# A four-direction Mamba block with two quantized FFNs: where the C rows live, and when the next step's work is issued

## The chip, the core and the metric

The kernel runs on one core of a Trainium2 chip. A core has five engines with a queue each: TensorE (PE in the profile; its weight loads are PEld), VectorE (DVE), ScalarE (ACT), GpSimd (POOL) and the sync engine (SP), which here issues nearly all DMA transfers. The metric is the device time of one launch in microseconds (us), the median over runs.

## The reference, cut to what matters

Two images `x[2, 96, 128, 128]` pass through two layers. The first layer normalizes over channels and runs four Mamba scans: over the pixels row by row, the same backwards, column by column, and that backwards. The outputs are concatenated, projected by `fuse_w` and added to `x`. An FFN follows, whose products and sums are rounded to 8 and 16 bits. The second layer is a 3x3 convolution over the normalized image and another FFN. Nearly all time is in the four scans:

```python
# per direction: D_INNER = 192 channels, D_STATE = 16 states, L = 16384 positions
xc, z = jnp.split(x @ in_w.T, 2, axis=-1)
xc = silu(causal_conv_4_taps(xc) + conv_b)
xdbl = xc @ xproj_w.T                      # dt_raw (6), B (16), C (16) of each position
dt = softplus(dt_raw @ dt_w.T + dt_b)
A = -exp(A_log)
def step(h, t):                            # h[channel, state]
    dA = exp(dt_t[:, :, None] * A)
    h = dA * h + dt_t[:, :, None] * B_t[:, None, :] * u_t[:, :, None]
    y = einsum('bds,bs->bd', h, C_t)
y = (ys + Dp * xc) * silu(z)
out = y @ outp_w.T
```

## The kernel before, in words

For each image the kernel runs three stages: `normalize`, `mamba` and `ffn_and_conv`. The change touches only `mamba` and the layout of its weights.

`mamba` takes the directions in two pairs (0, 2) and (1, 3), `pi` 0 and 1. The two directions of a pair have 2x192 = 384 channels, which are three groups `g` of 128 partitions: group 0 belongs to the first direction, group 2 to the second, and group 1 holds 64 channels of each, interleaved partition by partition. A step is 512 positions of a pair; there are 32 steps per pair, 64 per image, 128 in all. A step has 24 units: 3 groups times 8 pairs of states. Two units whose states are neighbours share a quad, a tile of 128x4x512 elements (1 MB) that holds rows of B or of C for four states. Each row is the same for all channels of a direction, so a quad is a transfer from DRAM that repeats the rows over the partitions (L335).

For one unit:

- `b_part` (L339) multiplies a B quad by dt·u on GpSimd, for two units at once. Then L342 and L343 add the state at the step's entry: `entry` on ScalarE forms the decay of the first position (L303), GpSimd multiplies it by the stored state `hst` and adds it to the first column.
- `decay` (L349) computes exp(A·dt) on ScalarE, two states, into one of three PSUM tiles `da`.
- `scan` (L353) is a scan instruction on VectorE per state. Its result goes into `da`, or into the B quad if GpSimd will multiply it.
- `behind` comes one unit later: the product with C on VectorE (L441), or for the units in `BY_POOL` on GpSimd (L360); it is written over the C quad. Then ScalarE copies the last column into `hst` (L442).
- `sums` (L357) adds the products over the states on TensorE into the PSUM bank `y`, with an identity as weights. For a unit of GpSimd the sums are issued three units later.
- At the first unit of a group, `gated` (L364) multiplies the finished `y` of the group before by silu(z) on VectorE. `y` has one bank, so the next group's first matmul (L448) waits for the gate. `project` and `collect` follow some units later.

The next step's preparation, `prologue`, is spread between the units. Its list `at` gives each piece a place (unit, before or after the unit's scans), counted from the start of the step before: the load of the normalized input `xa` and `xb` (-3), convolutions with the input projection (`inproj`, L211, at 1, 5 and 9), `rows` for dt, B and C (12), their way to DRAM (14), dt (14 to 17), gates (7, 18, 21), SiLU and softplus, which need another function table. All matmuls of the preparation and of the projection go through one PSUM bank, `misc`: each waits until ScalarE has read out the one before.

Group 1's convolution and gate outputs are computed with the two directions in halves and then interleaved by two small transfers (`mix`, L256).

The order of the instructions on each engine is the order in which the program issues them (`in_order`). The buffers and the waits are set by the tile pools: a tile gets a buffer when an earlier tile is released, which is after the last use of that tile. A transfer on SP that has to wait for this holds up what is behind it. Before the change, B quads rotate over four buffers and are fetched three quads ahead (`B_AHEAD`), C quads over three, two ahead (`C_AHEAD`).

Of the kernel before, what the change touches and what calls it, by code (L numbers as in the profile page):

```python
# [10 lines left out]
F32 = mybir.dt.float32  # L11
# [12 lines left out]
T = 512  # L24
# [8 lines left out]
B_AHEAD = 3  # L33
C_AHEAD = 2
AHEAD = 2
BY_POOL = tuple((g, s) for g in range(3) for s in (0, 8))
# [5 lines left out]
def tile_metaformer(ctx: ExitStack, tc: tile.TileContext, a: dict, out: bass.AP):  # L42
# [142 lines left out]
    def mamba(acc, xnr, xnc):  # L185

        with ExitStack() as st:
            pool = lambda n, bufs, **kw: st.enter_context(tc.tile_pool(name=n, bufs=bufs, **kw))

            io, gen, one, mixp, two = (pool(*p) for p in (("io", 2), ("gen", 4), ("one", 1), ("mixp", 1), ("two", 2)))  # L190
# [4 lines left out]
            enter = one.tile([128, NG, S], F32, name="enter")  # L195
# [5 lines left out]
            def inproj(pi, g, w, src, taps):  # L201

                ps = misc()
                for k in taps:
                    se = {"start": k == taps[0], "stop": k == taps[-1]}
                    for d, rows, lo, hi in (
# [4 lines left out]
                        nc.tensor.matmul(ps[rows, :], w(PAIRS[pi][d], k, lo, hi), src[d][:, k : k + T], **se)  # L211
                return ps

            def prologue(pi, i, d):
# [17 lines left out]
                def conv(g):  # L232
                    d["ps"] = inproj(pi, g, lambda dd, k, lo, hi: inx[:, dd, k, lo:hi], src, (0, 1, 2, 3))

                def conv_out(g):
                    if g == 1:
                        d["xc"] = two.tile([128, NG, T], F32, name="xc")
                    t = mixed("xc") if g == 1 else d["xc"][:, g, :]
                    nc.scalar.activation(t, d["ps"], AF.Identity, bias=convb[:, pi, g : g + 1])  # L239

                def gate(g):
                    d["ps"] = inproj(pi, g, lambda dd, k, lo, hi: inz[:, dd, lo:hi], src, (3,))

                def gate_out(g):
                    if g == 1:
                        d["sz"] = two.tile([128, NG, T], F32, name="sz")
                    nc.scalar.copy(mixed("sz") if g == 1 else d["sz"][:, g, :], d["ps"])  # L247

                def mixed(name):
                    d["mix", name] = mixp.tile([128, T], F32, name="mix")  # L250
                    return d["mix", name]

                def mix(name):

                    for k in range(2):
                        nc.sync.dma_start(d[name][k:128:2, 1, :], d["mix", name][64 * k : 64 * k + 64, :])  # L256
# [44 lines left out]
                def entry(g):  # L301

                    nc.scalar.activation(enter[:, g, :], amat[:, pi, g, :], AF.Exp, scale=d["dt"][:, g, 0:1])  # L303

                first = pi == 0 and i == 0
                at = [(-3, 1, load), (3, 0, partial(mix, "xc")), (11, 0, partial(silu, "xc"))]
# [360 lines left out]
```

## Time and profile before

| What | Value |
|---|---|
| Median of 3 runs | 11546.39 us (11545.31 to 11548.33) |
| Profiled execution: time, span | 11556.77 us, 11555.0 us |
| Mean granted TensorE clock | 0.989 |
| TensorE, VectorE, ScalarE, GpSimd busy over the span | 90%, 90%, 68%, 84% |
| Moved by DMA | 3416.96 MB, mean 296 GB/s |
| Row quads from DRAM | 3072 transfers of 1024.0 KB |

Shares of the span are means over three kinds of stages. In the 40 slices of the page, GpSimd is at 9 tenths in the two long scan stages and at 1 or 2 in the FFN stages. A row of a group gives: source line, engine, operation, output and inputs, count, then busy time in us and the mean in ns of one, then the idle time of the engine before these instructions and what released them. A row of the timeline gives start and duration in us; `x2` means merged instructions, and brackets name an idle time and its releaser. A row of stretches gives the stretch, its length, busy time and count of PE, PEld, DVE, ACT and POOL, then the granted clock, the DMA engines' busy share and GB/s.

### The profile page before, as it was taken

The page shows a single profiled execution, that of the slowest core. Times are in us where ns is not written, and L with a number is a line of the kernel's source. Part 1 is how long each engine was busy: PE and PEld are TensorE (multiplying, and loading weights), DVE is VectorE, ACT ScalarE, POOL GpSimd, SP SyncE. Part 2 cuts the span into 40 slices and gives each one's busy share as a digit, 9 for nine tenths or more (in the row PEclk, how much of TensorE's full clock was granted, in tenths as well). Part 3 has the DMA queues.
Part 4 walks back from the last instruction along what each step waited for, and adds up shares of the span by engine and source line. Part 5 has one row for each costly group of instructions (what it writes and reads, how often), then busy time and mean ns, then how long its engine had stood idle before and what let it go on. Part 6 is the DMA issues. An engine that isn't in the chain of part 4 may idle for free. (4 is left out here: it accounts for less than half of the span.)

```text
span 11555.0 us, 94102 instructions
## 1 busy us (share of the span) xinstructions
PE 10435.0 (90%) x24208; PEld 3971.4 (34%) x24208; DVE 10421.6 (90%) x10127; ACT 7901.7 (68%) x13564; POOL 9672.3 (84%) x4700
## 2 busy tenths in 40 slices
PE   7999999999999999989989999999999999999899
PEld 2333333333333333333323333333333333333333
DVE  6999999999999999994469999999999999999944
ACT  6767767677677677665567677677676776776655
POOL 5999999999999999991159999999999999999911
PEclk8999999999999999999989999999999999999999
DMA  7888888888888888880068888888888888888800
GB/s 263 335 329 333 333 332 332 330 331 333 329 332 333 330 331 333 329 322 19 26 243 334 328 331 334 330 333 333 333 331 329 332 332 329 331 333 329 319 13 13
DMA packets 540755, 3416.96 MB, mean 296 GB/s; under 512 B 67532, under 2 KB 68652, under 8 KB 143832
## 3 DMA queue, kind: packets, MB, share of 16 engines
q1 hardware_dynamic: 539960, 3410.16, 76.8%
q8 instruction: 196, 3.21, 0.1%
q14 instruction: 343, 2.81, 0.1%
q0 software_dynamic: 256, 0.79, 0.0%
HBM read 3289.04 MB, written 54.53 MB: 289 GB/s over the span
## 5 line engine op out<-in xcount | busy, mean ns | idle before, releaser
L339 POOL TENSOR_TENSOR row<-dtu,row 128x2048 f32<-128x2048 f32 x1536 | 6948.9, 4524 | 283.3 <-DMA row<-bcd 281.6
L357 PE MATMUL y<-row,ident 128*128 128x512 f32 x12288 | 5690.6, 603 | 700.0 <-DVE row L441 699.9
L353 DVE TENSOR_TENSOR_SCAN da<-da,row 128x512 f32<-128x512 f32 x4608 | 5456.9, 1214 | 38.9 <-ACT da L349 5.2
L349 ACT ACTIVATE da<-dt,amat 128x512 f32<-128x512 f32 x6144 | 4246.9, 691 | 170.2
L357 PEld LDWEIGHTS y<-row,ident 128*128 128x128 f32 x12288 | 2256.8, 190 | 4008.4 <-issue 2243.5
L441 DVE TENSOR_TENSOR row<-da,row 128x1024 f32<-128x1024 f32 x2304 | 2776.7, 1205 | 70.2 <-DMA row<-bcd 70.0
L442 ACT COPY hst<-da 128x2 f32<-128x2 f32 x2304 | 368.9, 160 | 2652.2 <-DVE row L441 2649.3
L360 POOL TENSOR_TENSOR row<-row,row 128x1024 f32<-128x1024 f32 x768 | 1807.4, 2353 | 223.0 <-DVE row L353 147.5
L353 DVE TENSOR_TENSOR_SCAN row<-da,row 128x512 f32<-128x512 f32 x1536 | 1852.4, 1206 | 91.9 <-POOL row L339 84.1
L211 PE MATMUL misc<-xa,inx 96*64 96x512 f32 (+1 forms) x2048 | 946.1, 605 | 50.0 <-ACT mix L239 26.8
L211 PE MATMUL misc<-xb,inx 96*64 96x512 f32 (+1 forms) x2048 | 952.3, 608 | 33.6 <-ACT hst L442 24.2
L564 POOL TENSOR_TENSOR acc<-acc,y 96x512 f32<-96x512 f32 x128 | 147.4, 1151 | 991.5 <-DVE y L563 991.5
L298 POOL TENSOR_TENSOR dtu<-dt,xc 128x512 f32<-128x512 f32 x384 | 487.4, 1269 | 106.0 <-DMA xb<-xnc 99.8
L576 PE MATMUL pc<-pad,kw 96*96 96x512 f32 x1152 | 566.4, 593 | 0.0
L211 PEld LDWEIGHTS misc<-xa,inx 96*64 96x64 f32 (+1 forms) x2048 | 327.3, 165 | 581.2 <-issue 438.0
L448 PE MATMUL y<-xc,dmat 128*128 128x512 f32 x768 | 419.5, 628 | 103.6 <-DVE sz L364 103.6
L374 PE MATMUL misc<-sz,gmat 128*96 128x512 f32 x1024 | 484.1, 595 | 0.0
L284 PE MATMUL misc<-rows,dtw 12*128 12x512 f32 x768 | 434.3, 645 | 50.6 <-ACT dt L289 37.9
L364 DVE TENSOR_TENSOR sz<-y,sz 128x512 f32<-128x512 f32 x384 | 264.6, 689 | 229.5 <-PE y L357 198.0
L136 DVE TENSOR_TENSOR xq<-xm,rs 96x512 fp8e5<-96x512 f32 x128 | 87.9, 687 | 392.2 <-ACT rs L132 392.2
L211 PEld LDWEIGHTS misc<-xb,inx 96*64 96x64 f32 (+1 forms) x2048 | 316.5, 164 | 361.9 <-issue 214.1
L372 PE MATMUL misc<-acc,ident 96*96 96x512 f32 x512 | 387.6, 842 | 57.3 <-ACT sz L247 53.8
(76 smaller groups left out, 7449.9 us busy)
## 6 DMA issues: line engine op xcount, KB each, us to landing
row<-bcd SPq DMA_DIRECT2D x3072, 1024.0 KB, 7.4
xc<-mix SPq DMA_DIRECT2D x256, 128.0 KB, 5.4
sz<-mix SPq DMA_DIRECT2D x256, 128.0 KB, 8.9
xa<-xnr SPq DMA_DIRECT2D x124, 193.1 KB, 8.6
xb<-xnc SPq DMA_DIRECT2D x124, 193.1 KB, 8.7
bcd<-rows SPq DMA_DIRECT2D x128, 128.0 KB, 9.5
acc<-in_x_dram SPq DMA_DIRECT2D x16, 768.0 KB, 5.7
xnr<-xn SPq DMA_DIRECT2D x16, 768.0 KB, 4.3
```

The costliest lines, as they stand in the source:

```text
L211: nc.tensor.matmul(ps[rows, :], w(PAIRS[pi][d], k, lo, hi), src[d][:, k : k + T], **se)
L284: nc.tensor.matmul(d["ps"], w, d["rows"][0 : 2 * RK, :], start=True, stop=True)
L298: nc.gpsimd.tensor_tensor(dtu, d["dt"][:, g, :], d["xc"][:, g, :], ALU.mult)
L339: nc.gpsimd.tensor_tensor(b, d["dtu"][g][:, None, :].broadcast_to((128, 4, T)), b, ALU.mult)
L349: nc.scalar.activation(da[:, j, :], d["dt"][:, g, :], AF.Exp, scale=amat[:, pi, g, s + j : s + j + 1])
L353: nc.vector.tensor_tensor_scan(h[:, j, :], da[:, j, :], b[:, j, :], 0.0, ALU.mult, ALU.add)
L357: nc.tensor.matmul(y, ident, c[:, j, :], start=False, stop=s + j == S - 1)
L360: nc.gpsimd.tensor_tensor(c, h, c, ALU.mult)
L374: nc.tensor.matmul(d["po"], gmat[:, pi, 2 * g - 2 + k, :], d["yg"][g - 1 + k], start=False, stop=k == 1)
L441: nc.vector.tensor_tensor(c, h, c, ALU.mult)
L448: nc.tensor.matmul(y, dmat[:, pi, g, :], d["xc"][:, g, :], start=True, stop=False)
L576: nc.tensor.matmul(pc, kw[:, t, :], rows, start=t == 0, stop=t == 8)
```

## The change

- C has four fixed quads, `crow`, one for each four states. They are filled whole for group 0; for group 1 only partitions 64 to 127 are refilled (with the second direction's rows), for group 2 partitions 0 to 63. Each refill is issued two quads after the quad's use.
- Products are written over the B quad. B quads rotate over five buffers, four ahead, and are fetched after the unit's scans.
- Group 1 is laid out in two halves of partitions instead of interleaved: its B quad takes two transfers of 64 partitions, and the `mix` transfers go.
- The entry state: ScalarE multiplies the first column of the decay by `hst`, with two copies of 128x1 per unit, and the scan starts from 1. GpSimd's additions go.
- GpSimd multiplies 7 of 24 units by C: states 2 and 8 of each group and 4 of group 1 (before: 0 and 8).
- The next step's preparation is issued at other places: the load at -6, the convolutions at -3, -1 and 1, in halves of two taps before and after the unit's scans, rows at 6, dt at 8 to 10, softplus at 11, gates at 12, 14 and 16, SiLU at 5 and 21.

```diff
-B_AHEAD = 3
-C_AHEAD = 2
+B_AHEAD = 4
-BY_POOL = tuple((g, s) for g in range(3) for s in (0, 8))
+BY_POOL = tuple((g, s) for g in range(3) for s in (2, 8)) + ((1, 4),)
...
-                at = [(-3, 1, load), (3, 0, partial(mix, "xc")), (11, 0, partial(silu, "xc"))]
-                at += [(9, 0, partial(mix, "sz")), (31, 1, partial(silu, "sz"))]
-                at += [(12, 0, rows), (13, 1, rows_out), (14, 0, rows_to_dram)]
-                for g, k in ((1, 1), (0, 5), (2, 9)):
-                    at += [(k, 0, partial(conv, g)), (k + 1, 1, partial(conv_out, g))]
-                for g, k in ((1, 7), (0, 18), (2, 21)):
+                at = [(-6, 1, load), (5, 1, partial(silu, "xc")), (21, 1, partial(silu, "sz"))]
+                at += [(6, 0, rows), (7, 1, rows_out), (8, 0, rows_to_dram)]
+                for g, k in ((1, -3), (0, -1), (2, 1)):
+                    at += [(k, 0, partial(conv, g, (0, 1))), (k, 1, partial(conv, g, (2, 3))), (k + 1, 1, partial(conv_out, g))]
+                for g, k in ((1, 12), (0, 14), (2, 16)):
                     at += [(k, 0, partial(gate, g)), (k + 1, 0, partial(gate_out, g))]
-                soft = ((0, 1, 16), (1, 3, 26)) if first else ((0, 3, 17),)
-                for x0, x1, k in soft:
-                    at += [(k, 1, partial(softplus, x0, x1))]
-                for g, k in enumerate((14, 24, 25) if first else (14, 15, 16)):
-                    at += [(k, 0, partial(dt_in, g)), (k + 1, 0, partial(dt_out, g))]
-                for g, k in enumerate((19, 27, 29)):
+                for g in range(NG):
+                    at += [(8 + g, 0, partial(dt_in, g)), (9 + g, 0, partial(dt_out, g))]
+                at += [(11, 1, partial(softplus, 0, NG))]
+                for g, k in enumerate((13, 24, 26) if first else (13, 17, 21)):
                     at += [(k, 0, partial(dt_u, g))]
-                    if i > 0:
-                        at += [((20, 24, 29)[g], 1, partial(entry, g))]
...
+            def row_tile(d, g, s):
+
+                t = gen.tile([128, 4, T], F32, name="row", bufs=B_AHEAD + 1)
+                for part, k in (((slice(0, 64), 0), (slice(64, 128), 1)) if g == 1 else ((slice(0, 128), g // 2),)):
+                    src = d["bcd"][0, s // 4, k]
+                    nc.sync.dma_start(t[part], src[None].broadcast_to((part.stop - part.start, 4, T)))
                 return t
+            crow = [one.tile([128, 4, T], F32, name=f"crow{q}") for q in range(S // 4)]
+
+            def c_fill(n, g, q):
+
+                if n < len(steps):
+                    part = (slice(0, 128), slice(64, 128), slice(0, 64))[g]
+                    src = state[n]["bcd"][1, q, int(g > 0)]
+                    nc.sync.dma_start(crow[q][part], src[None].broadcast_to((part.stop - part.start, 4, T)))
...
+                if i > 0:
+                    for j in range(2):
+                        nc.scalar.activation(da[:, j, 0:1], da[:, j, 0:1], AF.Copy, scale=hst[:, g, s + j : s + j + 1])
                 return da
-            def scan(j, da, b, h):
-                nc.vector.tensor_tensor_scan(h[:, j, :], da[:, j, :], b[:, j, :], 0.0, ALU.mult, ALU.add)
+            def scan(i, j, da, b, h):
+                nc.vector.tensor_tensor_scan(h[:, j, :], da[:, j, :], b[:, j, :], float(i > 0), ALU.mult, ALU.add)
...
-                    nc.vector.tensor_tensor(c, h, c, ALU.mult)
+                    nc.vector.tensor_tensor(b, h, c, ALU.mult)
...
                 if k % 2 == 0:
-                    fetch(k + 2 * B_AHEAD, 0, B_AHEAD, bs)
                     feed(k + AHEAD)
...
                 if k % 2 == 0:
-                    fetch(k + 2 * C_AHEAD, 1, C_AHEAD, cs)
+                    fetch(k + 2 * B_AHEAD)
+                    if 4 <= k < total + 4:
+                        cn, cu = divmod(k - 4, nu)
+                        cg, cq = cu // 8, cu % 8 // 2
+                        c_fill(cn + (cg == 2), (cg + 1) % 3, cq)
                 issue(k, 1)
```

The weights' layout follows (no permutation of group 1), and the program's scratch for software DMA is set to 4096 bytes.

## The prediction

> **What bounds the kernel now.** I read the page, then the stretches, the groups, one step of the timeline, and the waits. The page and a stretch of 1000 us inside the scan stage:
>
> ```profile
> PE 10435.0 (90%) x24208; PEld 3971.4 (34%) x24208; DVE 10421.6 (90%) x10127; ACT 7901.7 (68%) x13564; POOL 9672.3 (84%) x4700
> 4000.00:5000.00 1000.00, 912.23 (x2106) 347.48 (x2106) 967.37 (x873) 701.82 (x1211) 939.76 (x456) 1.00 0.86 331
> ```
>
> In the stage VectorE is 96.7% busy, GpSimd 94%, TensorE 91%, the DMA engines 86%. The chain of waits shows the same `y` piece at 8521.24 and at 10818.34, 29 steps apart: 79.2 us a step, so 128 steps are 10,138 of the 11,555 us. The groups:
>
> ```profile
> L353 DVE TENSOR_TENSOR_SCAN da<-da,row 128x512 f32<-128x512 f32 x4608 | 5456.9, 1214 | 38.9 <-ACT da L349 5.2 <-POOL row L339 0.8 <-ACT hst L442 0.8
> L441 DVE TENSOR_TENSOR row<-da,row 128x1024 f32<-128x1024 f32 x2304 | 2776.7, 1205 | 70.2 <-DMA row<-bcd 70.0
> L364 DVE TENSOR_TENSOR sz<-y,sz 128x512 f32<-128x512 f32 x384 | 264.6, 689 | 229.5 <-PE y L357 198.0 <-ACT hst L442 16.5 <-ACT mix L247 13.0
> L343 POOL TENSOR_TENSOR row<-row,enter 128x4 f32<-128x4 f32 x1488 | 298.3, 200 | 116.6
> L342 POOL TENSOR_TENSOR enter<-enter,hst 128x16 f32<-128x16 f32 x372 | 82.3, 221 | 0.0
> ```
>
> VectorE's largest idle time stands before the gate (L364), which waits for a group's last sums. Queues within one step:
>
> ```profile
> 8529.55 1.21 DVE L441 TENSOR_TENSOR row<-da,row 128x1024 f32<-128x1024 f32 x1
> 8530.67 2.33 DVE L353 TENSOR_TENSOR_SCAN da<-da,row 128x512 f32<-128x512 f32 x2
> 8580.44 0.69 DVE L364 TENSOR_TENSOR sz<-y,sz 128x512 f32<-128x512 f32 x1 [1.15 <-PE y L357]
> 8521.24 5.42 PE L357 MATMUL y<-row,ident 128*128 128x512 f32 x12 [1.38 <-DVE row L441]
> 8553.82 3.70 PE L211 MATMUL misc<-xb,inx 96*128 96x512 f32 x8 [0.44 <-ACT hst L442]
> 8580.70 1.28 ACT L293 ACT_TABLE_LOAD   x1
> 8524.98 15.52 SPq L335 DMA_DIRECT2D row<-bcd  x5
> ```
>
> VectorE issues an operation every 1.12 us (the end is 1.21 after the start), a gate takes 0.60. The sums of one unit are 4 records: 1.75. A four-tap convolution of 8 records takes 3.44 (half: 1.72), group 1's of 16 took 3.6. ScalarE's function changes (load, softplus or SiLU, load) take 4.1. The sync queue's waits in the same 80 us, and a quad's landing:
>
> ```profile
> SPq L335 <- PE y L357: 54.0, 11, 9.4
> DMA to landing us min/median/max: 4.1/7.4/17.9
> ```
>
> The queue stands 54 of 80 us on TensorE's sums: a quad's buffer is refilled only when its sums are done. A step needs 48 scans, 18 products, 3 gates: 66×1.12+1.8 = 75.7; 3.5 us are stalls.
>
> [...]
>
> **The change, part by part.** *VectorE*: 17 products: −1.12 us a step. Also, unit s=0 is no longer GpSimd's, so a product of 1.12 stands between a group's last sums and its gate; that could remove the gate's waits (198.0+16.5+13.0)/128 = 1.8. *GpSimd*: one more product (+2.35), without 12 row and 3 state operations ((298.3+82.3)/128 = −3.0): −0.6, hidden, as VectorE hardly waits for it. The mix transfers (0.5 MB, four SP issues) go: hidden.
>
> *ScalarE*: two 128x1 copies per unit behind the exponentials. [...]I take 0.5 us per unit. Ends: 0.2 (two row copies stood 0.08 from the next operation) and 0.6. A decay (state copy 0.2, exponentials 1.42, copies 0.5) is 2.1; in steady state it hides in waits of 1.1 to 1.8, not behind a function change.
>
> *DMA*: C falls from 12 to 8 MB a step; B for group 1 goes in two 64-partition transfers, C refills for groups 1 and 2 in one each. A single quad's minimum of 4.1 is about 1.5 fixed plus 2.6 per MB. Half transfers lie between full rate (1.3 per half) and half rate (2.6); no row decides, I take 1.75.
>
> *At nothing.* rows, dt, softplus and gate projections come 4 to 10 units sooner, with the same instructions: their results had time before (rows to DRAM landed four units ahead of the first B quad). If that cover went, a B quad would be late, which four quads ahead (before: three) make less likely. At the start of each batch 8 quads are loaded, not 5: at most 2×3×2.6 = 16 us, hidden behind the first quads' use. The four B quads that stand over from step to step now also hold the products, so a slot comes free after the sums, where before a B slot waited for VectorE or ScalarE only: this is the added wait. Behind it on SP stand the C refill, once a step the x windows, and rows to DRAM; TensorE, VectorE and GpSimd wait for these in turn.
>
> *Order* decides. In the changed instruction order each B refill waits for sums (TensorE), and C refills and the x windows stand behind it on SP. I follow a step from gate to gate, clock zero at each gate.
>
> Group 2 (units 17 to 24). Product 19 starts at 0.6+7×1.12 = 8.5, ends 9.7; its sums end at 11.5. Only then SP issues: a B quad, a half C refill, then xa and xb (0.39 MB), whose convolution stands next on TensorE. Landing 1.5+2.6+1.75+1.0 = 6.85: 18.4. TensorE stands still, then runs in order: convolution 22.0, sums 21 23.8, half convolution 25.5, sums 22 27.3, half 29.0, GpSimd's sums 20 30.7, sums 23 32.5; gate at 32.6. VectorE would have been there at 0.6+22×1.12 = 25.2. Before, this load had four units' time.
>
> Group 0 (units 1 to 8). TensorE: half convolution 1.7, D product 2.7, sums 0 4.4, half 6.1, ScalarE's output 6.8, projection (3.5) 10.3, sums 2 and 3 13.8. Then SP is free for B (two halves) and, behind it, the C quad for units 6 and 7: 1.5+3.5+2.6 = 7.6, so 21.5. Product 6 was due at 0.6+15×1.12 = 17.4; seven operations later the gate, 29.4 instead of 25.2. TensorE gives 29.1: SiLU of xc is done at 17.5 (collect till 12.7, a decay, 2.8 of the function), then rows 20.1, sums 5, 6, 4, one dt product, sums 7.
>
> Group 1 (units 9 to 16, three of them GpSimd's, 24.1 for VectorE). ScalarE: decay 11 till 2.1, dt output, decay 12, dt output, decay 13 till 7.4, softplus till 11.5, decay 14 ready at 13.4; its scan was due at 11.8: 25.7.
>
> Sum 29.4+25.7+32.6 = 87.7 against 79.2: +8.5 a step, ×128 = +1088. The profiled execution took 11,556.8 (span 11,555.0), the runs' median is 11,546.4, 0.1% less: I add to the median: **12,635 us**. Halves at full rate: 28.5+25.7+32.1 = 86.3, 12,455. At half rate 31.1+26.6+33.4 = 91.1, 13,070. Copies at 0.2 take 1.2 off group 1: 12,480; at 0.6, 0.4 more: 12,685.
>
> **Rivals.** *Milder, the x windows are not late.* If they land by 13, TensorE's next wait is ScalarE: product 19 9.7, decay 22 11.8, collect 12.3, decay 23 14.3, SiLU 18.4, decay 24 20.5, the output that frees the one misc bank 21.1; then half, sums 22, half, sums 20, sums 23 (8.7): gate 29.9. Sum 85.0: 12,290; with copies of 0.2, 82.9: 12,020. For it: 4.1 us landings exist. Against: three transfers stand ahead of xb.
>
> *Faster, VectorE stays the bound.* Product and gate waits go: −2.9 a step, 11,175. For it: VectorE's 96.7%, and 1.12 us more before each gate. It decides at one place: the convolution ahead of group 2's gate must start by 25.2−14.1 = 11.1 (3.6+1.75+8.7 of TensorE work follow), so SP must be free by about 4.3 where I find 11.6. If the sync queue really gets a slot that early, this wins; 54 of 80 us waiting speak against.
>
> *No change*: gains and waits of 2.9 cancel. *Worse*: DMA at half rate also delays GpSimd's C in group 1; above 13,150.
>
> **How the numbers follow.** Likeliest, both late transfers and the softplus stall: 0.58, its own range 12,350 to 13,150. Milder 0.22, 11,900 to 12,350. Worse 0.05, no change 0.04, faster 0.11. The range 11,900 to 13,150 holds 0.80. Within 0.2% is what a measurement tells from no change: faster 0.11, same 0.04, slower 0.85.
>
> **What would show it.** TensorE's group for xa or xb should wait on their DMA some 5 us a step (before: 18.1+4.6 us in all). The gate's wait for `y` should rise from 198 us to about 900 (7 a step); the products' wait for C, which was 70 us, to about 500. VectorE should fall to some 86% in the stage, POOL too. [...] I am wrong if the xa wait stays under 1 us a step, if SP is released before product 19's sums, or if VectorE keeps 96%.

## The result, and the profile after

| | before | after |
|---|---|---|
| Median of 4 runs | 11546.12 us | 14558.68 us (14525.29 to 14566.8) |
| Ratio | | 1.260, 95% interval 1.258 to 1.262 |
| VectorE, GpSimd in the stretch 4000 to 5000 us | 967, 940 us | 734, 706 us |
| Moved by DMA | 3416.96 MB | 2813.17 MB |

Slower, as forecast, but by 3,012 us instead of 1,088, and beyond the range. The page and the same stretch of the changed kernel:

```profile
PE 11532.2 (79%) x24208; PEld 4493.1 (31%) x24208; DVE 10387.0 (71%) x9999; ACT 8972.8 (62%) x19138; POOL 9607.7 (66%) x2968
4000.00:5000.00 1000.00, 781.83 (x1601) 306.57 (x1602) 734.37 (x655) 616.12 (x1351) 706.44 (x212) 0.88 0.70 207
```

No engine is near its limit in the stage, and the DMA engines are busy for 70% while they move 207 GB/s, against 86% and 331 before. VectorE did about the same work in all (10,387 against 10,422 us); the 3,012 us are idle time. The groups, with what ended their idle time in the last field:

```profile
L338 DVE TENSOR_TENSOR_SCAN row<-da,row 128x512 f32<-128x512 f32 x1792 | 2139.3, 1206 | 528.4 <-ACT da L334 520.4
L424 DVE TENSOR_TENSOR row<-da,crow 128x1024 f32<-128x1024 f32 x2176 | 2632.1, 1210 | 1640.9 <-DMA crow<-bcd 1637.8
L349 DVE TENSOR_TENSOR sz<-y,sz 128x512 f32<-128x512 f32 x384 | 265.1, 690 | 1008.5 <-PE y L342 1008.0
L334 ACT ACTIVATE da<-da,hst 128x1 f32<-128x1 f32 x5952 | 1149.7, 232 | 96.3
```

The products' wait for C rose from 70 to 1,638 us, the gate's wait for `y` from 198 to 1,008. The third wait of VectorE, 520 us, is for a decay that ScalarE makes late; the lines below show why. They are group 2 of one step, from the gate of group 1 at 5050.69 to its own at 5088.64 (start, duration, engine and line; the bracket is the idle time before):

```profile
5062.59 0.33 SPq L312 DMA_DIRECT2D row<-bcd  x1
5063.45 0.58 SPq L227 DMA_DIRECT2D xa<-xnr  x1
5071.21 1.09 PE L211 MATMUL misc<-xa,inx 96*64 96x512 f32 x1 [6.97 <-DMA xa<-xnr]
5076.35 1.03 PE L211 MATMUL misc<-xa,inx 96*64 96x512 f32 x1
5077.50 0.59 PE L211 MATMUL misc<-xb,inx 96*64 96x512 f32 x1
5078.14 0.69 ACT L237 ACTIVATE xc<-misc,convb 128x512 f32<-128x512 f32 x1 [7.14 <-PE misc L211]
5080.77 1.22 DVE L338 TENSOR_TENSOR_SCAN row<-da,row 128x512 f32<-128x512 f32 x1 [4.26 <-ACT da L334]
5088.64 0.69 DVE L349 TENSOR_TENSOR sz<-y,sz 128x512 f32<-128x512 f32 x1 [5.53 <-PE y L342]
```

This is the predicted sequence of group 2: the sync queue is free 11.9 us after the gate (predicted 11.6), the x windows go out, TensorE stands for 7 us and then does the convolution ahead of the sums. Two terms are larger. The windows' matmul starts 8.6 us after the queue was free, not 6.85. The 16 records of the convolution (they overlap) then take 6.8 us, not 3.6: each of the first thirteen lasts over 1 us, and only the last few 0.6. The granted clock, third number from the end, shows it too; the stretches are one before TensorE stood and one after:

```profile
5050.00:5060.00 10.00, 8.03 (x18) 2.71 (x16) 9.28 (x9) 5.21 (x14) 8.64 (x4) 1.00 0.92 289
5071.00:5075.00 4.00, 3.79 (x9) 2.19 (x11) 4.00 (x4) 0.00 (x0) 4.00 (x2) 0.50 0.99 402
```

The granted clock was 1.00 in the first stretch and 0.50 in the second. The same shows in all 16 waits of this sort between 3,000 and 5,400 us (TensorE stood for 6.3 to 10.3 us): slow records follow, and end 3.7 to 7.0 us after the first matmul. From the convolution's end at 5078.03 to the gate the trace has 10.6 us, and the prediction had 10.6.

VectorE's wait for the decay has the same origin. ScalarE stood 7.14 us for the convolution's result (L237), and the decay was queued behind that. The copies (L334) are only the last instructions of the decay.

C lands late in all three groups. Group 0, group 1 for VectorE and for GpSimd, and group 2:

```profile
5104.25 1.08 SPq L312 DMA_DIRECT2D row<-bcd  x2
5113.71 1.22 DVE L424 TENSOR_TENSOR row<-da,crow 128x1024 f32<-128x1024 f32 x1 [6.46 <-DMA crow<-bcd]
5041.38 1.23 DVE L424 TENSOR_TENSOR row<-da,crow 128x1024 f32<-128x1024 f32 x1 [3.42 <-DMA crow<-bcd]
5026.51 2.35 POOL L345 TENSOR_TENSOR row<-row,crow 128x1024 f32<-128x1024 f32 x1 [2.39 <-DMA crow<-bcd]
5070.78 1.22 DVE L424 TENSOR_TENSOR row<-da,crow 128x1024 f32<-128x1024 f32 x1 [2.30 <-DMA crow<-bcd]
```

In group 0 C lands for product 6, 9.5 us after the queue came free (predicted 7.6). In group 1, where only a softplus stall was predicted, C halves are late for VectorE and for GpSimd. The gates stand 31.1 (group 1), 37.95 (group 2) and 34.65 us (group 0) apart; predicted were 25.7, 32.6 and 29.4. The step is a usual one: from 3,000 to 5,400 us the means are 31.5, 37.8 and 34.1.

### The profile page after: what moved, and what is told of

Its sections match the earlier page's. It is cut to its first block, busy times and chain, and to the rows that moved or that the text cites. A ratio compares the mean times of both kernels' runs of the same rounds, so it can differ in the third digit from the quotient of the medians.

```text
span 14559.6 us, 97190 instructions
## 1 busy us (share of the span) xinstructions
PE 11532.2 (79%) x24208; PEld 4493.1 (31%) x24208; DVE 10387.0 (71%) x9999; ACT 8972.8 (62%) x19138; POOL 9607.7 (66%) x2968
## 2 busy tenths in 40 slices
DMA packets 442475, 2813.17 MB, mean 193 GB/s; under 512 B 67532, under 2 KB 68652, under 8 KB 111064
## 4 chain that ended last, share of the span: by engine, by line
PE 45%; DMA 22%; POOL 11%; DVE 9%; issue 6%; ACT 5%; SPq 2%; POOLq 0%; DVEq 0%; ACTq 0%
PE y L342 22%; DMA crow<-bcd 17%; PE misc L211 12%; POOL row L325 6%; DMA xa<-xnr 5%; POOL row L345 4%; DVE da L338 4%; PE pc L563 3%; DVE row L424 2%; DVE row L338 2%; SPq L312 2%; ACT da L331 2%; PE xm L121 1%; PE v L127 1%; PE misc L359 1%
## 5 line engine op out<-in xcount | busy, mean ns | idle before, releaser
L342 PE MATMUL y<-row,ident 128*128 128x512 f32 x12288 | 6385.8, 661 | 1480.0 <-issue 722.7
L338 DVE TENSOR_TENSOR_SCAN da<-da,row 128x512 f32<-128x512 f32 x4352 | 5172.1, 1215 | 292.6 <-POOL row L325 171.6
L345 POOL TENSOR_TENSOR row<-row,crow 128x1024 f32<-128x1024 f32 x896 | 2104.4, 2349 | 3136.0 <-ACT hst L425 2799.6
L342 PEld LDWEIGHTS y<-row,ident 128*128 128x128 f32 x12288 | 2524.4, 212 | 5215.8 <-issue 4503.7
L424 DVE TENSOR_TENSOR row<-da,crow 128x1024 f32<-128x1024 f32 x2176 | 2632.1, 1210 | 1640.9 <-DMA crow<-bcd 1637.8
L338 DVE TENSOR_TENSOR_SCAN row<-da,row 128x512 f32<-128x512 f32 x1792 | 2139.3, 1206 | 528.4 <-ACT da L334 520.4
L211 PE MATMUL misc<-xa,inx 96*64 96x512 f32 (+1 forms) x2048 | 1314.8, 791 | 857.2 <-DMA xa<-xnr 625.8
L211 PE MATMUL misc<-xb,inx 96*64 96x512 f32 (+1 forms) x2048 | 1280.4, 772 | 8.1 <-DMA xb<-xnc 4.8
L334 ACT ACTIVATE da<-da,hst 128x1 f32<-128x1 f32 x5952 | 1149.7, 232 | 96.3
L237 ACT ACTIVATE xc<-misc,convb 128x512 f32<-128x512 f32 x384 | 264.0, 688 | 1487.0 <-PE misc L211 1487.0
L255 PE MATMUL misc<-xc,bcw 128*96 128x512 f32 x768 | 427.1, 700 | 247.6 <-ACT xc L248 247.6
## 6 DMA issues: line engine op xcount, KB each, us to landing
crow<-bcd SPq DMA_DIRECT2D x512, 1024.0 KB, 10.6
```

What stands on the lines that cost most here:

```text
L211: nc.tensor.matmul(ps[rows, :], w(PAIRS[pi][dd], k, lo, hi), src[dd][:, k : k + T], **se)
L255: nc.tensor.matmul(d["ps"][0 : BCO + NBC, :], bcw[:, pi, g, :], d["xc"][:, g, :], start=g == 0, stop=g == NG - 1)
L334: nc.scalar.activation(da[:, j, 0:1], da[:, j, 0:1], AF.Copy, scale=hst[:, g, s + j : s + j + 1])
L338: nc.vector.tensor_tensor_scan(h[:, j, :], da[:, j, :], b[:, j, :], float(i > 0), ALU.mult, ALU.add)
L342: nc.tensor.matmul(y, ident, c[:, j, :], start=False, stop=s + j == S - 1)
L345: nc.gpsimd.tensor_tensor(h, h, c, ALU.mult)
```

## The experiments

All times are those of one profiled execution each, beside one of the kernel before on the same chip (11,543 to 11,554 us), except the last two, which are medians of 13 and 5 runs. Four runs of the changed kernel span 14,525 to 14,567 us, so a difference of 0.3% between single runs says nothing. Each quoted text is what was expected before the run.

**From the changed kernel: three undo one suspect each.** The theory was that the sync queue's late release, with half transfers of uncertain rate behind it, makes C and the x windows late. Below, "queue theory" stands for the late release alone, and "port theory" for the author's supposition that a transfer over 64 adjacent partitions is slow in itself, which no row of before shows.

a_ports: half transfers over 64 adjacent partitions replaced by the same bytes over all 128 (so group 1 and C hold other rows). The lines for C change in the same way:

```diff
-                for part, k in (((slice(0, 64), 0), (slice(64, 128), 1)) if g == 1 else ((slice(0, 128), g // 2),)):
+                for part, k in (((slice(0, 2), 0), (slice(2, 4), 1)) if g == 1 else ((slice(0, 4), g // 2),)):
...
-                    nc.sync.dma_start(t[part], src[None].broadcast_to((part.stop - part.start, 4, T)))
+                    nc.sync.dma_start(t[:, part], src[None].broadcast_to((128, part.stop - part.start, T)))
...
```

> The changed kernel; each transfer of 64 partitions is replaced by one of the same 0.5 MB over all 128 partitions (two of the four rows; the other rows are left as they are, so group 1 and the C rows of groups 1 and 2 get wrong data). Same number of transfers, same bytes, same order and waits. Port theory (64 adjacent partitions halve the rate, and this is what came on top of the forecast): a half refill lands in 5 to 6 us instead of 9.2, GpSimd's wait for C in group 1 goes, and the time falls to what the forecast gave for halves at full rate, about 12,450 us, to 13,000 us. Queue theory (the late release of B slots alone makes the waits): within 3% of 14,559 us.

Measured: 13,498, 1,061 us less and between the two theories. The half refill of C lands in 7.4 us (9.2 in the changed kernel), the products' wait for C falls to 717 us, GpSimd's (274 us in the changed kernel) goes, and the x windows stay late (679).

a_cfirst: C's refill issued ahead of the B fetch:

```diff
-                    fetch(k + 2 * B_AHEAD)
                     if 4 <= k < total + 4:
...
                         c_fill(cn + (cg == 2), (cg + 1) % 3, cq)
+                    fetch(k + 2 * B_AHEAD)
```

> The changed kernel; on the sync queue each C refill is issued ahead of the B quad of the same unit instead of behind it. Nothing else, same bytes. Queue theory: the refill no longer waits for the sums that free a B slot; VectorE's wait for C (1637.8 us, 12.8 us a step) falls below 300 us, and the time to 13,000 to 13,600 us. Port theory: the data volume at half rate is the same, so the waits move to the B quads and the time stays above 14,100 us.

Measured: 13,210, 1,349 us less, as the queue theory had it. A half refill takes even longer to land (11.1 us), but it is issued early enough: the products' wait for C falls to 5.5 us. The gate's wait stays (1,021).

a_load: the load six units sooner:

```diff
-                at = [(-6, 1, load), (5, 1, partial(silu, "xc")), (21, 1, partial(silu, "sz"))]
+                at = [(-12, 1, load), (5, 1, partial(silu, "xc")), (21, 1, partial(silu, "sz"))]
...
```

> The changed kernel; the load of the x windows is issued at -12 instead of -6, away from the B quad that waits for the sums of group 2. Nothing else. Queue theory: TensorE's wait for xa (625.8 us) goes, group 1's convolution runs in about 3.6 us instead of 6.9, the gate's wait for y falls below 500 us, and the time by 7 to 10 us a step to 13,300 to 13,700 us. Port theory: the next late refill takes its place, and the time stays above 14,200 us.

Measured: 13,610, 948 us less, again the queue theory's range. The wait for xa falls to 17.5 us, a record of the convolution from 791 to 619 ns on average, VectorE's wait for the decay (L334) in group 2 from 520 us to at most 32, and the gate's wait for `y` to 638 (not below 500); C stays late (1,617). So the late windows cost 7.4 us a step, and TensorE's slow records and the late decay came with them.

Which group gains tells what each was late for. These are mean times between gates, from 3,000 to 5,400 us of each trace:

| us | group 0 | group 1 | group 2 | Step |
|---|---|---|---|---|
| Before | 26.8 | 26.9 | 25.4 | 79.2 |
| Predicted | 29.4 | 25.7 | 32.6 | 87.7 |
| Changed kernel | 34.1 | 31.5 | 37.8 | 103.4 |
| Transfers over 128 partitions (a_ports) | 31.1 | 26.8 | 36.9 | 94.7 |
| C's refill first (a_cfirst) | 29.9 | 27.6 | 35.0 | 92.5 |
| Early load (a_load) | 32.8 | 31.5 | 30.7 | 95.0 |

Group 2 is late for the x windows. Group 1 is late for C's refills, and most of that goes with either of the other two runs: it takes both the order and the slow halves. Group 0 gains with both as well.

**Half transfers alone, on the kernel before (b_halves).** The B and C quads of group 1 go in halves, which are as many halves as in the changed kernel (2,048):

```diff
...
-                nc.sync.dma_start(t, src[None].broadcast_to((128 // n, n, 4, T)))
+                for part, n in (((slice(0, 64), 0), (slice(64, 128), 1)) if g == 1 else ((slice(0, 128), g // 2),)):
+                    src = d["bcd"][k, s // 4, n]
+                    nc.sync.dma_start(t[part], src[None].broadcast_to((part.stop - part.start, 4, T)))
```

> The kernel before; only group 1's quads of B and C are each loaded by two transfers of 64 adjacent partitions instead of one over 128 (the weights stay interleaved, so group 1 gets rows of the wrong direction). Port theory: 8 MB a step at half rate add 8 x 2.6 = 21 us of DMA time to a step of 79.2 us at 86% DMA, so the DMA engines become the bound at about 86 to 92 us a step: 12,400 to 13,200 us. Queue theory (half transfers cost no more than whole ones): 11,500 to 11,700 us.

Measured: 13,441, or +1,887, more than the port theory's range, with as many bytes to move. Between gates group 1 takes 41.6 us instead of 26.9; groups 0 and 2, whose quads stay whole, keep their 26.8 and 25.4. The stretch, GpSimd's product and VectorE's product, and the transfers by size with their median landing:

```profile
4000.00:5000.00 1000.00, 812.30 (x1763) 307.94 (x1761) 815.36 (x732) 598.54 (x1021) 792.86 (x383) 0.94 0.92 279
L339 POOL TENSOR_TENSOR row<-dtu,row 128x2048 f32<-128x2048 f32 x1536 | 6938.9, 4518 | 2021.7 <-DMA row<-bcd 1943.9
L441 DVE TENSOR_TENSOR row<-da,row 128x1024 f32<-128x1024 f32 x2304 | 2781.3, 1207 | 1284.0 <-DMA row<-bcd 1282.6
row<-bcd SPq DMA_DIRECT2D x2048, 1024.0 KB, 7.5
row<-bcd SPq DMA_DIRECT2D x2048, 512.0 KB, 12.7
```

The DMA engines are busier (0.92 against 0.86) and move less (279 against 331 GB/s), and a half quad takes longer to land than a whole one (median 12.7 against 7.5 us). Share times step, the engines are busy for some 86 us a step (0.92 of 93.8 us) instead of 68 (0.86 of 79.2). By this estimate the 8 MB of halves, a third of the bytes, took some 40 us of the engines' time instead of 22, 18 us more, where the port theory had 21; this in a kernel that already used 86% of its DMA engines. The rival, that two transfers cost more than one whatever their partitions, was tested in the changed kernel alone: there as many transfers over 128 partitions (a_ports) took 1,061 us less.

**Repairs together.** C first and the early load (a_cl); then the transfers over 128 partitions as well (a_pcl); then, in place of those, group 1 interleaved as before with its `mix` transfers and one B transfer, and C's halves as every second partition (best1):

```diff
-                    part = (slice(0, 128), slice(64, 128), slice(0, 64))[g]
+                    part = (slice(0, 128), slice(1, 128, 2), slice(0, 128, 2))[g]
```

> The changed kernel with both moves of order: C refills ahead of the B quad, and the load at -12. Half transfers as they are. If the two waits add (each sits in its own group of the step): 14,559 - 1,349 - 948 = 12,260, 12,100 to 12,500 us. Port theory: the same bytes at half rate are then the bound, DMA busy near 90% in the scan stage, and the time stays above 12,800 us.

> The changed kernel with both moves of order and with every transfer of 64 partitions replaced by one of the same bytes over 128 (wrong rows in group 1 and its C). If queue order and ports are the whole cause, nothing else in the change costs much: 11,200 to 11,800 us, VectorE over 93% busy in the scan stage. If the earlier preparation or ScalarE's copies cost by themselves: above 12,000 us.

> The changed kernel with both moves of order and group 1 interleaved again as before, with the mix transfers; B of group 1 is one transfer, and a C refill of half a quad writes every second partition, 64 partitions over the whole range. Port theory (adjacent partitions are what is slow): a half refill lands as fast as in the run with full-range transfers, and the time is 11,200 to 11,800 us. If any 64-partition transfer is slow: above 12,000 us.

Measured: 12,707, 12,670 and 12,671. So the forecasts by which order, load and ports were the whole cause failed: some 1,120 us are left. C's halves land in 7.3 us as every second partition and in 7.7 over all 128, so the every-second form isn't slow. With halves of adjacent partitions (a_cl) they land in 11.5, and the DMA engines are busy for 83% of the stretch instead of 64% (a_pcl), at the same 243 GB/s. Once order and load are right, the half transfers cost at most 0.3%, and group 1's interleaving, `mix` transfers included, nothing that shows. What is left in the second of them:

```profile
DVE sz L349 <- PE y L342: 1042.6, 254, 5.4
PE misc L255 <- ACT xc L248: 351.8, 128, 3.6
```

The gate waits once for each of two groups a step, some 4 us each. TensorE stands before the `rows` matmuls (L255) for SiLU of xc, and before the half convolutions for ScalarE's outputs, with the last sums of the group queued behind. That is the preparation at its new places.

**The places: put back, and alone.** o_old is best1 with the preparation at the old places and convolutions whole (load at -6; the old lines of `at` are in the diff of the change):

> This is the repaired kernel best1 (group 1 interleaved as before, C refills ahead of the B fetch, halves of every second partition) with one thing put back: the next step's preparation at the places of the kernel before, convolutions whole (1, 5, 9), rows at 12, dt from 14, softplus at 17, gates at 7, 18, 21, SiLU at 11 and 31; the load stays at -6. Theory A (what is left of the loss, some 1,120 us, comes from the preparation's new places: the half convolution ahead of group 2's gate and the rows ahead of group 0's): 11,300 to 11,700 us, and the gate's wait for y falls from about 1,000 us to below 400. Theory B (the fixed C quads and the products in the B quads keep it slow, whatever the places): above 12,300, with the gate's wait for y near 1,000 or the products' wait for C in its place.

Measured: 12,162, between the two theories: 509 of the 1,120 us go. On the kernel before, all new places alone (b_prep); and only the load, the convolutions in halves and the first mix transfer at new places, with rows, dt, gates, softplus and SiLU at the old (b_conv; its diff):

```diff
-                at = [(-3, 1, load), (3, 0, partial(mix, "xc")), (11, 0, partial(silu, "xc"))]
+                at = [(-6, 1, load), (11, 0, partial(silu, "xc")), (31, 1, partial(silu, "sz"))]
+                at += [(-1, 0, partial(mix, "xc")), (9, 0, partial(mix, "sz"))]
...
-                for g, k in ((1, 1), (0, 5), (2, 9)):
-                    at += [(k, 0, partial(conv, g)), (k + 1, 1, partial(conv_out, g))]
+                for g, k in ((1, -3), (0, -1), (2, 1)):
+                    at += [(k, 0, partial(conv, g, (0, 1))), (k, 1, partial(conv, g, (2, 3))), (k + 1, 1, partial(conv_out, g))]
```

> The kernel before with one part of the change alone: the next step's preparation at its new places, convolutions in halves of two taps (load -6, mix transfers at -1 and 14, rows 6, dt 8 to 10, softplus 11, gates 12, 14, 16, SiLU 5 and 21). Theory A (the places themselves cost, by TensorE's queue ahead of two gates): 12,300 to 12,800 us, the gate's wait for y 700 us or more instead of 198. Theory B (the places cost only because the sync queue is late in the changed kernel): within 150 us of before, 11,400 to 11,700, the gate's wait for y near 200.

> The kernel before with the load at -6, the convolutions in halves at -3, -1 and 1 and nothing else of the new places: rows, dt, softplus, gates and SiLU stay at the old ones. Alone, all new places cost 1,709 us. Theory A (it is the convolution behind a load only three units ahead, TensorE standing and then slow, and halves between group 2's last sums and the gate): 12,500 to 12,900 us, a wait for xa of 400 us or more. Theory B (it is the rest: rows and dt in group 0, three gates and the softplus in group 1): below 12,000, with the wait for xa under 200 us.

Measured: 13,252 (+1,709), more than theory A allowed, and 12,742 (+1,192), in theory A's range (its wait for xa is 372 us). The waits of the first:

```profile
POOL row L338 <- DMA row<-bcd: 1896.2, 572, 20.3
DVE sz L363 <- PE y L356: 1591.9, 381, 7.2
PE misc L213 <- DMA xa<-xnr: 461.4, 112, 9.2
```

So even with the buffers of before, a load at -6 doesn't reach a convolution at -3. The gate waits for TensorE, and GpSimd's wait for rows rose from 282 to 1,896 us. B is fetched on the same queue as C, whose buffers come free only after the sums, and that queue's wait for sums rose from 6,879 to 8,181 us; that this is the link was not tried apart. About 500 of the 1,709 belong to the places of rows, dt, gates and functions, which the prediction had set at nothing. In the first run TensorE waits 338 us, once a step, for SiLU of xc before `rows`; in the second 7 us in all.

a_old is the changed kernel with the old places alone (the same lines of `at`, without the mix transfers):

> The changed kernel with one part undone: the preparation at the places of the kernel before, convolutions whole (the load stays at -6); half transfers, the B fetch ahead of the C refill, the copies and the seven products of GpSimd stay. Alone, on the kernel before, the new places cost 1,709 us, the copies 417 and half transfers 1,887, of a loss of 3,012: the parts overlap. Theory A (the places make the x windows late and fill TensorE's queue; the two late transfers of C in groups 0 and 1 are left): 13,000 to 13,500 us, no wait for xa to speak of, the products' wait for C still above 1,000 us. Theory B (once the sync queue frees the C refills late, the places matter little, since each group waits for one thing only): 13,900 to 14,500.

Measured: 13,782, 777 us less, again between the theories: no wait for xa is left to speak of, the products' wait for C is 1,754 us.

**The copies: taken away, and alone.** a_nocopy is the changed kernel without ScalarE's copies, each step's scan starting from zero, so that the entry state is left out:

```diff
-                if i > 0:
+                if i > NT:
...
-                nc.vector.tensor_tensor_scan(h[:, j, :], da[:, j, :], b[:, j, :], float(i > 0), ALU.mult, ALU.add)
+                nc.vector.tensor_tensor_scan(h[:, j, :], da[:, j, :], b[:, j, :], 0.0, ALU.mult, ALU.add)
```

> The changed kernel without ScalarE's two copies per unit and with scans that start from 0 (the state at a step's entry is left out). Queue and port theories: the copies are hidden in the other waits, 14,300 to 14,600 us. Copy theory (they hold up every decay and so the outputs that free the misc bank): below 14,100 us.

Measured: 14,752, 1.3% more, where neither theory had more than 14,600. VectorE's wait for ScalarE's decay is nearly as long as with them (469 against 520 us, now from the exponential), as it must be if it comes from the late convolution, and the waits for C and xa grew (to 1,734 and 858). b_entry is the kernel before with the copies alone, in place of GpSimd's additions:

```diff
-                    nc.gpsimd.tensor_tensor(b[:, :, 0], b[:, :, 0], enter[:, g, s : s + 4], ALU.add)
...
+                        nc.scalar.activation(da[:, j, 0:1], da[:, j, 0:1], AF.Copy, scale=hst[:, g, s + j : s + j + 1])
...
```

> The kernel before with one part of the change alone: the entry state by ScalarE's two 128x1 copies per unit and scans that start from 1, without GpSimd's additions. Theory A (the copies hide in ScalarE's waits and GpSimd's relief of 3.0 us a step hardly matters): 11,450 to 11,600 us. Theory B (the copy needs the stored state, so a decay now waits for the scan of a step before only, never late, but 0.39 us per unit makes ScalarE late behind its function changes): 11,750 to 12,100, with VectorE's scans waiting for the decay by 200 us or more. Theory C (GpSimd was close to the bound and its relief is a gain): 11,150 to 11,400.

Measured: 11,961, +417, in theory B's range, though the scans' direct wait for the decay is 120 us and not 200. VectorE's waits in it:

```profile
DVE sz L361 <- PE y L354: 408.4, 231, 6.2
DVE da L350 <- ACT da L346: 119.7, 122, 1.0
DVE row L438 <- DMA row<-bcd: 113.2, 117, 2.0
```

The copies are a direct wait once a step (L346), and most of the rest arrives through the gate (408 us against 198). In the changed kernel they don't show; the likely reason is that VectorE stood anyway. A way without either: the scan takes the stored state as its initial value (b_ptr).

```diff
-                nc.vector.tensor_tensor_scan(h[:, j, :], da[:, j, :], b[:, j, :], 0.0, ALU.mult, ALU.add)
+                e = hst[:, g, s + j : s + j + 1] if i > 0 else 0.0
+                nc.vector.tensor_tensor_scan(h[:, j, :], da[:, j, :], b[:, j, :], e, ALU.mult, ALU.add)
```

> The kernel before with the entry state given to the scan itself, as its initial value (a column of the stored state), so with neither ScalarE's copies nor GpSimd's additions. In the same place the copies cost 417 us. Theory A (the 417 us are ScalarE's own time, 0.39 us a unit on the way to a decay): 11,400 to 11,560 us, the scans' wait for a decay below 60 us; a scan stays near 1,215 ns. Theory B (they are lost since GpSimd, without its additions, starts its products sooner and its B products later): near 11,900 again. Theory C (a scan with an initial value from memory is dearer): each 0.1 us more in a scan's mean is 0.1 x 48 x 128 = 614 us.

Measured: 11,753, +203. The waits for a decay are gone, but such a scan is dearer:

```profile
L348 DVE TENSOR_TENSOR_SCAN da<-da,hst,row 128x512 f32<-128x512 f32 x4464 | 5548.3, 1273 | 14.7 <-ACT hst L437 1.1 <-ACT da L343 0.4
4000.00:5000.00 1000.00, 898.36 (x2063) 337.81 (x2062) 982.67 (x857) 680.04 (x1151) 888.26 (x262) 0.99 0.84 324
```

1,273 against 1,214 ns is 0.059 x 5,952 = 351 us on the engine that sets the pace. VectorE is at 98.3%. Theory C names the cost that the trace shows, and by its own rule it would be 351 us; 203 were lost, so some 150 came back elsewhere. The runs tell no more of where within ScalarE's queue the 417 us are lost.

**What is left: fixed C quads, the states, the seventh product.** o_old6 is o_old with GpSimd's six old units; o_ptr7 is o_old with the scan above. The first as a diff:

```diff
-BY_POOL = tuple((g, s) for g in range(3) for s in (2, 8)) + ((1, 4),)
+BY_POOL = tuple((g, s) for g in range(3) for s in (0, 8))
```

> As o_old, and GpSimd multiplies the 6 units of the kernel before (states 0 and 8 of each group) instead of 7. Theory A1 (the seventh unit is a gain for VectorE, 1.12 us a step, 143 us, and state 2 in place of 0 puts a product of VectorE's between the last sums and the gate): 100 to 400 us slower than o_old. Theory A2 (GpSimd, 94% busy in the stage before, is the next bound, and its seventh product of 2.35 us makes the B products late): 50 to 300 us faster than o_old.

> As o_old (fixed C quads refilled ahead of the B fetch, group 1 interleaved, preparation at the old places, seven products of GpSimd), with the entry state as the scan's initial value in place of the copies. o_old took 12,162, and the copies cost 417 on the kernel before. Theory A (the copies cost as much here, and GpSimd with 3.0 us less a step carries its seventh product): 11,350 to 11,750 us. Theory B (GpSimd's seventh product makes B late whatever ScalarE does; o_old waited 618 us for it): 11,800 to 12,150, the scans' wait for GpSimd's row still above 400 us.

Measured: 11,970 (192 less than o_old: the seventh product and the other states together cost that much) and 11,966. In the second VectorE still waits 500 us for GpSimd's `row`, so its theory B holds. Then the core of the change alone: the kernel before with fixed C quads, halves of every second partition refilled ahead of the B fetch, products over the B quads, load at -6. Without (o_gp6) and with (o_gp28) the change's choice of states 2 and 8:

```diff
-C_AHEAD = 2
+B_AHEAD = 4
...
+                    part = (slice(0, 128), slice(1, 128, 2), slice(0, 128, 2))[g]
+                    src = state[n]["bcd"][1, q, int(g > 0)]
+                    nc.sync.dma_start(crow[q][part], src[None].broadcast_to((64 if g else 128, 4, T)))
...
```

> The kernel before with the fixed C quads alone: C filled whole for group 0 and by halves of every second partition for groups 1 and 2, refills ahead of the B fetch, products over the B quads, five B buffers; the entry by GpSimd, six products of GpSimd at states 0 and 8, the preparation at the old places (load at -6). o_old6, the same with ScalarE's copies, took 11,970; the copies cost 417 on the kernel before. Theory A (fixed C quads cost nothing in themselves; a third of C's bytes less leaves the waits for C and B): 11,450 to 11,570 us, a ratio of 0.992 to 1.002. Theory B (B slots that come free only after the sums make B late): 11,650 to 12,000, with GpSimd waiting for row and VectorE for the gate's y.

> As o_gp6, with GpSimd's six products at states 2 and 8 of each group, as in the changed kernel, in place of 0 and 8. Theory A (a product of VectorE's then stands between a group's last sums and the gate, and hides the gate's wait of 1.8 us a step): 100 to 230 us faster than o_gp6. Theory B (state 2's sums come later in the group, behind the projection, and the gate isn't what holds VectorE): within 60 us of o_gp6.

Measured: 11,541.6 (ratio 0.9992, 95% interval 0.9984 to 1.0), theory A, and 11,784.8 (1.0198, 1.0185 to 1.0212), slower where both of its theories had none or a gain. The stretch and the gate's wait of the first, then what VectorE waits for in the second:

```profile
4000.00:5000.00 1000.00, 908.59 (x2105) 343.97 (x2103) 967.28 (x872) 701.70 (x1211) 939.28 (x455) 1.00 0.73 279
DVE sz L370 <- PE y L363: 245.0, 252, 3.2
```

```profile
DVE da L359 <- POOL row L349: 422.1, 397, 2.4
DVE da L359 <- POOL row L345: 79.0, 13, 34.9
```

Fixed C quads lower the DMA engines' share from 0.86 to 0.73 and change no time: VectorE is at 96.7% as before, and DMA wasn't the bound. With states 2 and 8 the gate's wait falls to 6 us, as the prediction's gain of 1.8 us a step had it, but GpSimd's B products come late, which costs more. These 243 us are more than the 192 above, so what the seventh product costs or saves by itself stays open.

The parts then add up along one path (us; each step is a run above, mostly a single one, and the runs of the kernel before beside them differ by up to 10 us):

| Step | Time | Added |
|---|---|---|
| before | 11,551 | |
| fixed C quads (o_gp6) | 11,542 | -9 |
| ScalarE's copies in place of GpSimd's additions (o_old6) | 11,970 | 429 |
| states 2 and 8, seventh product (o_old) | 12,162 | 192 |
| new places, load at -12 (best1) | 12,671 | 509 |
| half transfers of adjacent partitions, no mix (a_cl) | 12,707 | 35 |
| load at -6 (a_cfirst) | 13,210 | 503 |
| B fetch ahead of C's refill (after) | 14,559 | 1,349 |

Along another path the shares differ (halves alone on before: 1,887, here 35): a wait cost little where others stood in its place. No version ran faster than before by more than its measurement tells: o_gp6 is within 0.2%.

## Why the prediction was right and wrong

The forecast was 87.7 us a step; the step shown took 103.7. The missing 16 us are spread evenly: 5.25 in group 0, 5.4 in group 1, 5.35 in group 2. The measured time lies in the range of the rival "worse", which had 0.05.

- *Direction, and the places of the two late transfers: right.* C behind the B fetch and the late x windows are what the prediction followed; undoing them gains 1,349 and 948 us. Its rival "faster" set its own test, a queue free by 4.3 us; the trace has 11.9.
- *Group 1: the step that failed.* The prediction let group 1's C land in time and gave the group nothing but a softplus stall. In the runs that stall is absent (VectorE waits 0.1 us a step for a decay there), and C's halves are late instead, in the step shown by 2.4 us for GpSimd and 3.4 for VectorE. With C's refill first, or with transfers over 128 partitions, the group falls from 31.5 to 27.6 or 26.8 us. The 500 us predicted for the products' wait for C were 1,638: all three groups waited, where one was counted. Only the rival "worse" had seen C late in this group.
- *The rate of half transfers: a term mis-sized.* Between full and half rate the prediction's sums differ by 615 us (12,455 to 13,070), and it took a value nearer to full rate. Replacing them gained 1,061 us. The median landing of a half was 7.8 us (B) and 9.2 us (C); the landings had been built from the minimum of a single quad, 4.1 us, with 1.75 for each half ahead. The split of the 4.1 into 1.5 and 2.6 was the author's estimate, and so were both rates and the 1.75: no row of before shows a half. In b_halves the halves took some 1.8 times as long on the DMA engines (40 against 22 us), near the half rate.
- *Group 2: mechanism right, two terms mis-sized.* The queue came free 0.3 us later, the landing took 8.6 instead of 6.85, and "convolution 22.0" used a duration from a TensorE that had not stood: 6.8 instead of 3.6. Together these are 5.3 of the group's 5.35.
- *Group 0: mechanism right, two terms mis-sized.* The queue was free at 15.6 (predicted 13.8), C landed after 9.5 (7.6), and 1.5 more are waits before the last product and the gate.
- *"At nothing" was wrong for the earlier places.* The prediction asked only whether their results would be ready in time. Their matmuls stand in TensorE's queue ahead of the sums, and `rows` waits there for ScalarE's SiLU. On the kernel before this cost about 500 us (13,252 less 12,742); in the repaired kernel all new places together, convolutions included, cost 509.
- *Copies.* The size, 0.5 us per unit, was the author's assumption, taken from no trace (measured 0.39, with 232 ns for a copy). In the changed kernel, leaving them out gains nothing. But "in steady state it hides" fails in a kernel without other stalls: there they cost 417 us.
- *Removals at nothing:* nothing speaks against it. With group 1's interleaving and its mix transfers the repaired kernel takes 12,671, without them 12,670, but these two differ in their C transfers too. One product less for VectorE was not seen apart.
- *The added wait on the B slots* costs nothing in itself: o_gp6 has it. It did harm through what stood behind it on the queue (1,349 us with the B fetch ahead of C's refill), which is what the prediction said of order.
- *Checks*: the wait for xa and xb is 4.9 us a step (predicted 5), the gate's for `y` 1,008 us (900), VectorE is busy for 73% of the stretch (86%). That the first two came so close is partly luck. TensorE's whole idle time before the matmuls of xa is 857 us, 6.7 a step, of which 626 are put down to the DMA; and of the gate's wait group 2 has 5.55 us a step, where the prediction had all of its 7.

## What to carry to other kernels

Write down, for each transfer that moves behind a waiting one, when the queue comes free, what it lands behind, and what its first user has queued behind it; do this for every group, not only for those where a stall is expected. Price work after a stall with durations that come after stalls (here 6.8 us for a convolution, not 3.6), and put the transfer that is needed first ahead of the one with slack. A part that alone is free (fixed C quads) can bring with it an order of transfers that costs 1,349 us.

## What the runs showed that was not expected

- Two transfers of 64 adjacent partitions in place of one of 128, same bytes: +1,887 us on a kernel with busy DMA engines (median landing 12.7 us for a half), but 37 us in the repaired kernel, where other waits stood in their place (12,707 against 12,670). Halves of every second partition landed in 6.1 to 7.3 us (medians of the runs that have them).
- Matmul records of 1.06 us instead of 0.6 for some 6 us after TensorE had stood for 7, at a granted clock of 0.50; in 16 such stalls 3.7 to 7.0 us.
- The scan whose initial value is a column in memory took 59 ns more than one that starts from a constant (1,273 against 1,214 ns).
- Work taken away from ScalarE in a kernel that stands on DMA made it 1.3% slower (one run); why is open.
